# A graph layer on one core: the maxima of the turned tiles go to ScalarE, which then copies 84 columns a chunk, and the sums are cleared by a bitwise and

## The chip, the cores and the metric

One Trainium2 chip, one of its cores. The metric is the device time of one execution in microseconds (us); lower is better. The engines are named as in the profile: PE is TensorE (PEld its weight loads), DVE is VectorE, ACT is ScalarE, POOL is GpSimd, and SP is SyncE, which here only issues DMAs. Each engine runs its own instruction stream in order. The letter q behind an engine's name (ACTq, DVEq, SPq) marks what the engine's sequencer does by itself: it loads registers, waits for semaphores, issues DMAs, and hands the other instructions to the engine.

## The reference

One message-passing layer of a graph network. There are 12,500 nodes with 48 numbers each, and 400,000 edges with 32 numbers each; the edges are sorted by their destination.

```python
h = jnp.maximum(_layernorm(x, axis=-1), 0.0)
tmp = jnp.concatenate([h[dst], h[src], edge_attr], axis=1)     # 48 + 48 + 32
m = jax.nn.relu(tmp @ W1 + b1) @ W2 + b2                       # 128 hidden, 48 out
x = x + jax.ops.segment_sum(m, dst, num_segments=12500)
```

All of it is in fp32, and the output is the 12,500 x 48 array.

## The kernel before, in words

The first 95 us or so make the tables. The layer norm is applied, and the product with W1 is taken per node instead of per edge: `tab_a` has a row of 128 per node for the destination part, `tab_b` one for the source part, both in HBM. `bt` is `tab_b` turned, so that a node is a column of 128 partitions, and it stays in SBUF.

The main loop (`windows`) takes the edges in 391 chunks of 1024, a chunk being 8 tiles of 128 edges. For a chunk the kernel needs, edge by edge, the destination's row, the edge's own product and the source's row. The destinations of a chunk lie within 80 neighbouring nodes, so that a 0/1 matrix (`lhs`, made on DVE in L463), stacked on the edge numbers, gives the first two in one product with `rhs` (L481, into the PSUM tile `pre`). The sources are anywhere, and their rows come in one of three ways:

- most tiles: POOL gathers 128 rows of `tab_b` into `gb` by an indirect DMA (L452), and DVE adds them to `pre` (L517);
- the "turned" tiles: DVE and ACT copy 128 single columns of `bt` into a tile `gt`, one instruction per edge (L393), and PE adds the turned `gt` to `pre` (L491). A chunk has one or two turned tiles, 458 in all;
- 36 "single" tiles: SP issues one DMA per row into `gr` (L425), and DVE adds the tile (L515).

Then DVE takes the maximum with zero of the gathered tiles in place (`hidden`, L530, from `hid` to `hid`) and of the turned tiles (L532, from `pre` to `hid`). PE multiplies `hid` with a second 0/1 matrix `hot` (made in L469) and so folds a chunk into 80 columns (`fold`, L541; L546 counts the edges), and DVE adds these to a running array of sums `seg` in SBUF (`add`, L560). Every 12 chunks a segment of `seg` is done: PE multiplies it with W2 (L586, L587), DVE adds that to the node's `x` (L588), and SP stores it (L592). The array of the segment after next is cleared by two MEMSETs (L576), and the columns that reach over are copied (L578).

Which column a copy reads is a number in a register. `PARTS` sets how many columns are copied in a chunk, and by whom: four parts of 19, 20, 16 and 16 on DVE, five of 16 on ACT. Each part is a `load` followed by its `columns`: one TENSOR_LOAD on the engine's own sequencer brings the part's numbers from the SBUF tile `last` into registers (L358), and the copies behind it use them. Chunk c's numbers are in partition c % 128 of `last`. In part 0 the load brings one number more than the part's columns: where in `seg` the chunk adds.

The order of the work is written out by hand (`manual_schedule`), as a software pipeline. In round c of the loop, DVE does `lhs` and `hot` of chunk c, the addition and the maxima of chunk c-1, and the `add` of chunk c-2; PE does `before` (the product of L481) of chunk c-1, `fold` of chunk c-2 and `turned` (L491) of chunk c-1, in this order; the copies of round c fill the tiles that `turned` takes from round c+1 on. The `gt` pool has 5 buffers, so ACT may run some rounds ahead of the others until it needs a `gt` buffer that PE has not yet read.

Of the kernel before, what the change touches and what calls it, by code (L numbers as in the profile page):

```python
# [36 lines left out]
STORE = 2  # L37
# [33 lines left out]
SEG0 = 130848  # L71
# [207 lines left out]
def windows(nc, tc, gp, bt, ident, idx, x_t, tab_a, tab_b, dst, edge_t, w1, w2s, b2s, out_t):  # L279
# [3 lines left out]
    with ExitStack() as es:  # L283
# [54 lines left out]

        rhss = []
# [14 lines left out]
        def numbers(c, at, n, engine):  # L354

            got = []
            for k in range(0, n, MOST):
                got += nc.values_load_multi_w_load_instructions(  # L358
                    last[c % P : c % P + 1, c // P, at + k : at + min(k + MOST, n)],
# [40 lines left out]
        def mark(ins, us):  # L400
            marks.append((ins, us))
# [28 lines left out]
        def prepare(c):  # L430
# [9 lines left out]
            lhs = ld.tile([P, CE], F32, name="lhs")  # L440
# [67 lines left out]
        def gathered(c):  # L508

            s = st[c]  # L510
            s["h"] = h = wp.tile([P, T, HID], F32, name="hid")
# [7 lines left out]
            for fetch in s["fetches"]:  # L519
                tc.declare_no_dep(  # L520
                    added.ins, fetch, reason="the product that is waited for waits for the rows"
                )
            mark(added, 1.0)
            spans[c], marks[:] = list(marks), []

        def hidden(c):
# [3 lines left out]
            mark(nc.vector.tensor_scalar(of, of, 0.0, None, op0=ALU.max), 0.55)  # L530
            if turned_at(c):
                nc.vector.tensor_scalar(  # L532
                    apart(c, s["h"], True), apart(c, s["pre"], True), 0.0, None, op0=ALU.max
                )
# [35 lines left out]

        def segment_next(g):

            old, new = segs[g % 2], segs[(g + 1) % 2]
            if g > 0:
                for k in range(2):
                    nc.vector.memset(new[:, k, W:], 0.0)  # L576
# [401 lines left out]
```

## Time and profile before

| what | value |
|---|---|
| median of 3 runs | 3527.61 us (3528.13, 3527.61, 3518.28) |
| the profiled execution: time | 3517.03 us |
| the profiled execution: span from its first to its last instruction | 3515.3 us |
| DVE busy | 3234.7 us (92%) |
| ACT busy | 3123.3 us (89%) |
| POOL busy | 2660.5 us (76%) |
| PE busy | 2616.9 us (74%) |
| granted PE clock, mean | 0.781 |

A profiled execution is one run with the hardware profiler. In its rows "x" stands before a count; behind the bar come the time in which at least one instruction of the group ran, the mean length of one in ns, and the idle time of the engine just before them with what ended it. Single-column copies overlap one another on their engine, so that their mean length is more than the step from one start to the next. A register load on a sequencer is not counted as busy time, and where an engine stands still for one, the profile calls the wait "issue".

### The profile page before, as it was taken

How to read it: one execution, taken by the hardware profiler on the slowest of the kernel's cores; microseconds unless marked ns; L12 is line 12 of the kernel's file. 1: busy time of each engine (PE TensorE's matmuls, PEld its weight loads, DVE VectorE, ACT ScalarE, POOL GpSimd, SP SyncE). 2: the span in 40 equal slices, each digit the busy share in tenths (PEclk: the TensorE clock that was granted, in tenths of full speed). 3: DMA queues.
4: the chain of work that ended last, by engine and by line, in shares of the span. 5: the costliest groups of instructions: out<-in, count | busy, mean ns of one | idle time of the engine just before them, and what ended most of it. 6: DMA issues, size and time to landing. Idle time of an engine off the chain costs nothing.

```text
span 3515.3 us, 119801 instructions
## 1 busy us (share of the span) xinstructions
PE 2616.9 (74%) x17111; PEld 2351.3 (67%) x17111; DVE 3234.7 (92%) x30218; ACT 3123.3 (89%) x31115; POOL 2660.5 (76%) x2658
## 2 busy tenths in 40 slices
PE   8677777777777776777777777777777777777777
PEld 5567666666676666666666766666667666676666
DVE  6799999999999999999999999999999999999997
ACT  5899998999998899989999899899999999898893
POOL 5777777777777777777777777777777777777775
PEclk9777777778777778778877787777777778778777
DMA  5533333333333333333333333333333333333332
GB/s 198 169 98 99 95 94 95 93 93 104 96 96 93 93 95 98 97 95 94 96 94 94 100 96 94 95 93 94 103 96 95 93 93 96 97 100 97 92 94 68
DMA packets 197238, 349.02 MB, mean 99 GB/s; under 512 B 67762, under 2 KB 104516, under 8 KB 195156
## 3 DMA queue, kind: packets, MB, share of 16 engines
q0 software_dynamic: 84224, 172.62, 19.3%
q1 hardware_dynamic: 111952, 168.56, 16.1%
q14 instruction: 658, 5.39, 0.5%
q8 instruction: 144, 2.36, 0.3%
q10 hardware_dynamic: 260, 0.10, 0.0%
HBM read 321.55 MB, written 22.07 MB: 98 GB/s over the span
## 4 chain that ended last, share of the span: by engine, by line
DVE 75%; PE 10%; ACT 5%; issue 4%; DVEq 3%; ACTq 0%; DMA 0%; SPq 0%
DVE gt L393 40%; DVE hid L517 9%; DVE hot L469 7%; DVE lhs L463 6%; DVE hid L530 6%; ACT gt L393 5%; PE p_g L541 4%; DVEq L358 3%; DVE seg L560 2%; DVE hid L532 2%; PE p_f L586 2%; PE p_f L587 2%; DVE xseg L588 1%; PE pre L491 1%; DVE seg L576 1%
## 5 line engine op out<-in xcount | busy, mean ns | idle before, releaser
L393 ACT COPY gt<-bt 128x1 f32 x31040 | 3076.9, 187 | 298.9 <-PE pre L491 195.5
L452 POOL DMA_INDIRECT gb<-tab_b,srci x2631 | 2639.0, 1003 | 821.8 <-issue 373.3
L393 DVE COPY gt<-bt 128x1 f32 x27584 | 1813.3, 143 | 147.6 <-issue 98.3
L541 PE MATMUL p_g<-hot,hid 128*128 128x80 f32 x6250 | 1069.5, 342 | 839.5 <-DVE hid L530 838.5
L541 PEld LDWEIGHTS p_g<-hot,hid 128*128 128x128 f32 x6250 | 1001.1, 251 | 913.1 <-DVE hid L530 903.5
L481 PEld LDWEIGHTS pre<-rhs,lhs 112*128 112x128 f32 x6250 | 963.0, 243 | 92.1 <-issue 91.6
L481 PE MATMUL pre<-rhs,lhs 112*128 112x128 f32 x6250 | 989.7, 326 | 20.0 <-DMA lhs<-in_edge_t 17.4
L517 DVE TENSOR_TENSOR hid<-pre,gb 128x896 f32<-128x896 f32 (+2 forms) x391 | 408.0, 1044 | 0.0
L469 DVE TENSOR_TENSOR hot<-wnum,rel 128x640 f32<-128x640 f32 x391 | 318.2, 814 | 0.0
L463 DVE TENSOR_SCALAR lhs<-row,bw 80x1024 f32<-80x1024 int16 x391 | 289.7, 741 | 10.0 <-DMA row<-in_dst 10.0
L491 PE MATMUL pre<-ident,gt 128*128 128x128 f32 x916 | 271.3, 404 | 17.5 <-issue 12.1
L530 DVE TENSOR_SCALAR hid<-hid 128x896 f32<-128x896 f32 (+2 forms) x391 | 244.9, 626 | 0.1
L546 PE MATMUL p_g<-hot,ones 128*128 128x80 bf16 x3125 | 240.0, 238 | 0.0
L546 PEld LDWEIGHTS <-ones 128*128 128x128 bf16 x3125 | 239.9, 132 | 0.0
L491 PEld LDWEIGHTS pre<-ident,gt 128*128 128x128 f32 x916 | 193.1, 269 | 20.1 <-issue 14.3
L560 DVE TENSOR_TENSOR seg<-seg,p_g 128x160 f32 x391 | 122.4, 313 | 7.5 <-issue 3.5
L532 DVE TENSOR_SCALAR hid<-pre 128x128 f32<-128x128 f32 (+1 forms) x389 | 118.0, 303 | 0.0
L588 DVE TENSOR_TENSOR xseg<-xseg,p_f 48x512 f32<-48x512 f32 (+1 forms) x67 | 45.0, 672 | 63.9 <-PE p_f L587 63.8
L586 PE MATMUL p_f<-seg,w2s 128*48 128x512 f32 (+1 forms) x134 | 102.8, 861 | 0.4 <-DVE seg L560 0.4
L587 PE MATMUL p_f<-seg,b2s 1*48 1x512 f32 (+1 forms) x134 | 90.7, 763 | 0.0
L587 PEld LDWEIGHTS p_f<-seg,b2s 1*48 1x48 f32 x134 | 12.6, 137 | 84.3 <-issue 83.1
L576 DVE MEMSET seg<- 128x944 f32 x64 | 54.1, 845 | 9.3
(67 smaller groups left out, 289.4 us busy)
## 6 DMA issues: line engine op xcount, KB each, us to landing
gr<-tab_b SPq DMA_DIRECT2D x4608, 0.5 KB
row<-in_dst SPq DMA_DIRECT2D x390, 160.0 KB
lhs<-in_edge_t SPq DMA_DIRECT2D x390, 128.0 KB
gb<-tab_b,srci POOLq DMA_INDIRECT x2631
rhs<-tab_a SPq DMA_DIRECT2D x391, 40.0 KB
xseg<-in_x_t SPq DMA_DIRECT2D x33, 192.0 KB
out_x<-xseg SPq DMA_DIRECT2D x33, 192.0 KB
tab_b<-tab SPq DMA_DIRECT2D x3, 1280.0 KB
```

The source lines that it names most:

```text
L393: done = copy(gts[of][:, e : e + 1], bt8[:, bass.ds(at, 4)].bitcast(F32))
L452: fetch = nc.gpsimd.indirect_dma_start(out=gb[:, t, :], out_offset=None, in_=tab_b[:, :], in_offset=bass.IndirectOffsetOnAxis(ap=srci[:, c ...
L463: mark(nc.vector.tensor_scalar(lhs[:W, : n * P], row[:, : n * P], bw[:, c : c + 1], None, op0=ALU.is_equal,), 0.8)
L469: mark(nc.vector.tensor_tensor(hot[:, :n, :], wnum.unsqueeze(1).to_broadcast([P, n, W]), rel[:, c * T : c * T + n].unsqueeze(2).to_broadca ...
L481: s["behind"] = nc.tensor.matmul(pre[:, t, :], s["lhs"][:K, t * P : (t + 1) * P], s["rhs"][:K, :], start=True, stop=t not in turned_at(c), ...
L491: s["behind"] = nc.tensor.matmul(s["pre"][:, t, :], gts.pop(j), ident, start=False, stop=True).ins
L517: added = nc.vector.tensor_add(to, of, rows)
L530: mark(nc.vector.tensor_scalar(of, of, 0.0, None, op0=ALU.max), 0.55)
L532: nc.vector.tensor_scalar(apart(c, s["h"], True), apart(c, s["pre"], True), 0.0, None, op0=ALU.max)
L541: nc.tensor.matmul(p_g[:, 0, :], s["h"][:, t, :], s["hot"][:, t, :], start=t == 0, stop=t == n - 1)
L546: nc.tensor.matmul(p_g[:, 1, :], ones, high[:, t, 1::2], start=t == 0, stop=t == n - 1)
L560: mark(nc.vector.tensor_add(to, to, s["p_g"]), 0.25)
```

## The change

The maxima of the turned tiles leave DVE: `hidden` keeps the gathered tiles, and the new `hidden_turned` is an ACTIVATE with Relu on ACT, from `pre` to `hid`. It runs one round later, in round c for chunk c-2, just before `fold` of that chunk, and on ACT it stands behind the first of ACT's parts. `hid` and `lhs` become three fixed tiles each instead of pool buffers. The parts become 15, 20, 20 and 20 on DVE (75) and 20, 16, 16, 16 and 16 on ACT (84), 159 columns a chunk instead of 151; with them there are 483 turned tiles instead of 458, 48 single tiles instead of 36 (`SINGLE` rows a chunk go from 12 to 16), and 2594 gathered ones instead of 2631. The `gt` pool has 8 buffers instead of 5. The numbers lie in 64 partitions instead of 128: `row_of` uses the first 16 of each 32. The sums are cleared by a `tensor_scalar` with a bitwise and with 0, one half each in the sixth and the eighth round of a segment, instead of two MEMSETs in its last round. The product of a finished segment with W2 (`segment_product`) and its addition (`segment_sum`) are now in different rounds, the addition one round later, and the store comes two rounds later. Line numbers shift: in the changed kernel the copies are L407, the loads L372, the Relu L556.

```diff
 BLK = 512
-STORE = 2
+STORE = 4
+CLEAR = 5
...
 PARTS = (
-    (True, 0, 19, 1),
-    (True, 19, 20, 20),
-    (True, 39, 16, 40),
-    (True, 55, 16, 56),
-    (False, 71, 16, 72),
-    (False, 87, 16, 88),
-    (False, 103, 16, 104),
-    (False, 119, 16, 120),
-    (False, 135, 16, 136),
+    (True, 0, 15, 1),
+    (True, 15, 20, 16),
+    (True, 35, 20, 36),
+    (True, 55, 20, 56),
+    (False, 75, 20, 76),
+    (False, 95, 16, 96),
+    (False, 111, 16, 112),
+    (False, 127, 16, 128),
+    (False, 143, 16, 144),
 )
...
-SINGLE = 12
-SINGLE_AT = 160
+SINGLE = 16
+SINGLE_AT = 168
...
+HALF_ROWS = 16
+USED = P // 2
+LAST = (NCH + 2 + USED - 1) // USED
+
+
+def row_of(c):
+
+    group, row = divmod(c % USED, HALF_ROWS)
+    return 2 * HALF_ROWS * group + row, c // USED
...
-        gtp = es.enter_context(tc.tile_pool(name="gtp", bufs=5))
-        wp = es.enter_context(tc.tile_pool(name="wp", bufs=3))
+        ld = es.enter_context(tc.tile_pool(name="ld", bufs=LOADS))
+        gtp = es.enter_context(tc.tile_pool(name="gtp", bufs=8))
+        wp = es.enter_context(tc.tile_pool(name="wp", bufs=HIDS))
...
+        lhss = [one.tile([P, CE], F32, name=f"lhs{k}") for k in range(LOADS)]
+        hids = [one.tile([P, T, HID], F32, name=f"hid{k}") for k in range(HIDS)]
...
+            row, slot = row_of(c)
             for k in range(0, n, MOST):
                 got += nc.values_load_multi_w_load_instructions(
-                    last[c % P : c % P + 1, c // P, at + k : at + min(k + MOST, n)],
+                    last[row : row + 1, slot, at + k : at + min(k + MOST, n)],
...
-            s["h"] = h = wp.tile([P, T, HID], F32, name="hid")
+            s["h"] = h = hids[c % HIDS]
...
+            if c - HIDS in relus:
+                tc.declare_no_dep(
+                    added.ins, relus.pop(c - HIDS),
+                    reason="the products that read this buffer last waited for that maximum",
+                )
...
         def hidden(c):
 
             s = st[c]
             of = apart(c, s["h"], False)
             mark(nc.vector.tensor_scalar(of, of, 0.0, None, op0=ALU.max), 0.55)
+
+        def hidden_turned(c):
+
             if turned_at(c):
-                nc.vector.tensor_scalar(
-                    apart(c, s["h"], True), apart(c, s["pre"], True), 0.0, None, op0=ALU.max
-                )
+                relus[c] = nc.scalar.activation(
+                    apart(c, st[c]["h"], True), apart(c, st[c]["pre"], True), AF.Relu
+                ).ins
...
+        def segment_clear(g, k):
+
+            new = segs[(g + 1) % 2][:, k, W:].bitcast(I32)
+            nc.vector.tensor_scalar(new, new, 0, None, op0=ALU.bitwise_and)
+
         def segment_next(g):
 
             old, new = segs[g % 2], segs[(g + 1) % 2]
-            if g > 0:
-                for k in range(2):
-                    nc.vector.memset(new[:, k, W:], 0.0)
...
-        def segment_sum(g, k, n):
+        out_of = {}
+
+        def segment_product(g, k, n):
 
             seg, s = segs[g % 2], slice(k * BLK, k * BLK + n)
-            p_f = ps_f.tile([D, BLK], F32, name="p_f")
+            out_of[g, k] = p_f = ps_f.tile([D, BLK], F32, name="p_f")
             nc.tensor.matmul(p_f[:, :n], w2s, seg[:, 0, s], start=True, stop=False)
             nc.tensor.matmul(p_f[:, :n], b2s[:1, :], seg[:1, 1, s], start=False, stop=True)
-            nc.vector.tensor_add(xs[g][:, s], xs[g][:, s], p_f[:, :n])
+
+        def segment_sum(g, k, n):
+
+            s = slice(k * BLK, k * BLK + n)
+            nc.vector.tensor_add(xs[g][:, s], xs[g][:, s], out_of.pop((g, k))[:, :n])
...
                 load(c, 1)
                 columns(c, 1)
+                g, k = group(c - 2)
+                if g > 0 and k in (1, 3):
+                    segment_sum(g - 1, k // 2, BLK)
+                load(c, DVE_PARTS)
+                columns(c, DVE_PARTS)
                 if 0 <= c - 1 < NCH:
                     before(c - 1)
                 if 0 <= c - 2 < NCH:
+                    hidden_turned(c - 2)
                     fold(c - 2)
                 if 0 <= c - 1 < NCH:
                     turned(c - 1)
-
-                g, k = group(c - 2)
+                if g > 0 and k in (0, 2):
+                    segment_product(g - 1, k // 2, BLK)
                 if k == GQ - 3 or c == NCH - 1:
                     segment_load(g)
-                if g > 0 and k < L // BLK:
-                    segment_sum(g - 1, k, BLK)
                 if g > 0 and k == STORE:
                     segment_store(g - 1, L)
                 if 0 <= c - 1 < NCH:
...
                 columns(c, 2)
                 if 0 <= c - 1 < NCH:
                     hidden(c - 1)
+                if g > 0 and k in (CLEAR, CLEAR + 2):
+                    segment_clear(g, (k - CLEAR) // 2)
                 load(c, 3)
                 if 0 <= c - 2 < NCH:
                     add(c - 2)
                     if k == GQ - 1:
                         segment_next(g)
                 columns(c, 3)
-                for part in range(DVE_PARTS, len(PARTS)):
+                for part in range(DVE_PARTS + 1, len(PARTS)):
                     load(c, part)
                     columns(c, part)
                 if c == NCH + 1:
+                    segment_sum(g - 1, 1, BLK)
+                    segment_store(g - 1, L)
+                    segment_product(g, 0, END_L)
                     segment_sum(g, 0, END_L)
                     segment_store(g, END_L)
```

What is left out is the place of the columns in `last` and how the host fills it.

How the instructions stand, first on ACT in the middle of the main loop, three parts before (`gt` with a number is one of its buffers, `last` the numbers, `bt` the turned table):

```order
L393 COPY gt_73753<-bt_58 128x1 x16
L358 TENSOR_LOAD last_87
L393 COPY gt_74185<-bt_58 128x1 x16
L358 TENSOR_LOAD last_87
L393 COPY gt_74185<-bt_58 128x1 x16
```

and in the changed kernel, from the end of one round's copies to behind the Relu of the next round:

```order
L372 TENSOR_LOAD last_87
L407 COPY gt_71927<-bt_58 128x1 x16
L372 TENSOR_LOAD last_87
L407 COPY gt_71927<-bt_58 128x1 x14
L407 COPY gt_72264<-bt_58 128x1 x6
L556 ACTIVATE hid0_716<-pre_71681 128x2x128
L372 TENSOR_LOAD last_87
L407 COPY gt_72264<-bt_58 128x1 x16
```

The parts of 16 alternate with loads as before; new are the part of 20 (here 14 and 6, since a `gt` buffer is full) and the Relu between it and the next load (128x2x128 where the chunk has two turned tiles, 128x128 where it has one).

On DVE, from the addition of the gathered rows to the next chunk's `lhs`, before:

```order
L517 TENSOR_TENSOR hid_109192<-pre_109164,gb_108437 128x2x384
L358 TENSOR_LOAD last_87
L393 COPY gt_108981<-bt_58 128x1 x16
L530 TENSOR_SCALAR hid_109192<-hid_109192 128x2x384
L532 TENSOR_SCALAR hid_109192<-pre_109164 128x2x128
L358 TENSOR_LOAD last_87
L560 TENSOR_TENSOR seg0_663<-seg0_663,p_g_109173 128x2x80
L393 COPY gt_108981<-bt_58 128x1 x16
L463 TENSOR_SCALAR lhs_109545<-row_109547,bw_85 80x1024
```

and in the changed kernel:

```order
L531 TENSOR_TENSOR hid0_716<-pre_115878,gb_115056 128x2x384
L372 TENSOR_LOAD last_87
L407 COPY gt_115578<-bt_58 128x1 x20
L551 TENSOR_SCALAR hid0_716<-hid0_716 128x2x384
L372 TENSOR_LOAD last_87
L584 TENSOR_TENSOR seg0_663<-seg0_663,p_g_115888 128x2x80
L407 COPY gt_115578<-bt_58 128x1 x20
L477 TENSOR_SCALAR lhs2_715<-row_116234,bw_85 80x1024
```

One instruction is gone between the maximum and the load behind it, and both parts there have 20 copies instead of 16.

More of the change, by code (lines that the diff above doesn't have):

```diff
@@ L36 @@
 BLK = 512
-STORE = 2
+STORE = 4
+CLEAR = 5
+HIDS = LOADS = 3
 NOUT = NPAD + L
@@ L55 @@
 PARTS = (
-    (True, 0, 19, 1),
-    (True, 19, 20, 20),
-    (True, 39, 16, 40),
-    (True, 55, 16, 56),
-    (False, 71, 16, 72),
-    (False, 87, 16, 88),
-    (False, 103, 16, 104),
-    (False, 119, 16, 120),
-    (False, 135, 16, 136),
+    (True, 0, 15, 1),
[7 more added lines that the diff above has]
+    (False, 143, 16, 144),
 )
 PART = sum(n for _, _, n, _ in PARTS)
-BASE = 152
+BASE = 160
 DVE_PARTS = sum(dve for dve, *_ in PARTS)
 BT0 = 16512
-SEG0 = 130848
+SEG0 = 133248
 SEG_SIZE = 8 * L
-SEG, NEXT, SEG2 = 153, 154, 155
-PLACE0 = 156
-SINGLE = 12
-SINGLE_AT = 160
-WIDTH = 172
+SEG, NEXT, SEG2 = 161, 162, 163
+PLACE0 = 164
+SINGLE = 16
+SINGLE_AT = 168
+WIDTH = 184
 SLOTS = (NCH + 2 + P - 1) // P
 MOST = 32
+HALF_ROWS = 16
[4 more added lines that the diff above has]
+    return 2 * HALF_ROWS * group + row, c // USED
 def tiles_of(first, part):
@@ L287, in windows @@
         one = es.enter_context(tc.tile_pool(name="wone", bufs=1))
-        ld = es.enter_context(tc.tile_pool(name="ld", bufs=3))
-        gtp = es.enter_context(tc.tile_pool(name="gtp", bufs=5))
-        wp = es.enter_context(tc.tile_pool(name="wp", bufs=3))
+        ld = es.enter_context(tc.tile_pool(name="ld", bufs=LOADS))
+        gtp = es.enter_context(tc.tile_pool(name="gtp", bufs=8))
+        wp = es.enter_context(tc.tile_pool(name="wp", bufs=HIDS))
         grp = es.enter_context(tc.tile_pool(name="grp", bufs=3))
@@ L439, in prepare @@
             )
-            lhs = ld.tile([P, CE], F32, name="lhs")
+            lhs = lhss[c % LOADS]
             nc.sync.dma_start(lhs[W:K, : n * P], edge_t[:, at : at + n * P])
@@ L522, in gathered @@
                 )
+            if c - HIDS in relus:
[3 more added lines that the diff above has]
+                )
             mark(added, 1.0)
             spans[c], marks[:] = list(marks), []
+        relus = {}
         def hidden(c):
@@ L819, in tile_gnn_preln @@
     flag = const.tile([1, 1], I32, name="flag")
-    last = const.tile([P, SLOTS, WIDTH], I32, name="last")
+    last = const.tile([P, LAST, WIDTH], I32, name="last")
     ones = const.tile([P, P], BF16, name="ones")
@@ L924 @@
     by_tile = src.reshape(NT, P)
-    numbers = np.zeros((SLOTS * P, WIDTH), np.int32)
+    numbers = np.zeros((LAST * USED, WIDTH), np.int32)
     first = dst[::CE]
@@ L942 @@
     numbers[COLS : COLS + len(rows), SINGLE_AT : SINGLE_AT + SINGLE] = rows
-    last = np.ascontiguousarray(numbers.reshape(SLOTS, P, WIDTH).transpose(1, 0, 2))
+    last = np.zeros((P, LAST, WIDTH), np.int32)
+    for c, row in enumerate(numbers):
+        at, slot = row_of(c)
+        last[at, slot] = row
     arrays = {
```

## The prediction

> **What bounds the kernel now.** First the page: how busy each engine is, the chain that ended last, and the costliest groups.
>
> ```profile
> span 3515.3 us, 119801 instructions
> PE 2616.9 (74%) x17111; PEld 2351.3 (67%) x17111; DVE 3234.7 (92%) x30218; ACT 3123.3 (89%) x31115; POOL 2660.5 (76%) x2658
> DVE 75%; PE 10%; ACT 5%; issue 4%; DVEq 3%; ACTq 0%; DMA 0%; SPq 0%
> L393 ACT COPY gt<-bt 128x1 f32 x31040 | 3076.9, 187 | 298.9 <-PE pre L491 195.5
> ...
> L393 DVE COPY gt<-bt 128x1 f32 x27584 | 1813.3, 143 | 147.6 <-issue 98.3
> ```
>
> DVE carries the chain, and ACT is close behind it. Then the waits, to see which engine has slack, and for whom it waits.
>
> ```profile
> ACT gt L393 <- PE pre L491: 195.5, 89, 6.5
> ...
> DVE gt L393 <- issue: 98.3, 388, 3.6
> ...
> DVE xseg L588 <- PE p_f L587: 63.8, 37, 9.2
> ```
>
> DVE waits for another engine in the loop only at the segments' additions (63.8 us). ACT's slack is 195.5 us: in 89 places it has run so far ahead that no `gt` buffer is free. Over 390 rounds that is 0.50 us a round, and this is what an addition to ACT may cost before ACT sets the pace. Two rows of the timeline give DVE's pace:
>
> ```profile
> 105.65 0.75 DVE L463 TENSOR_SCALAR lhs<-row,bw 80x1024 f32<-80x1024 int16 x1 [9.09 <-DMA row<-in_dst]
> ...
> 3487.32 0.54 DVE L463 TENSOR_SCALAR lhs<-row,bw 80x640 f32<-80x640 int16 x1
> ```
>
> (3487.32 - 105.65) / 390 = 8.67 us a round. The question for the change is whether DVE or ACT needs longer for its new round.
>
> **ACT's round now.** Three views of ACT: its copies in two narrow stretches, an undisturbed stretch early in the loop, and its loads by stretches of time.
>
> ```profile
> 2005.44 1.11 ACT L393 COPY gt<-bt 128x1 f32 x11
> ...
> 2006.58 0.56 ACT L393 COPY gt<-bt 128x1 f32 x5
> ...
> 102.56 23.85 ACT L393 COPY gt<-bt 128x1 f32 x240 [0.17 <-issue]
> 126.58 0.56 ACT L393 COPY gt<-bt 128x1 f32 x5 [0.17 <-issue]
> ```
>
> ```profile
> L393 ACT COPY gt<-bt x31040: 185/187/193, 94.5 to 3464.9; 128x1 f32 x199
> ...
> L358 ACTq TENSOR_LOAD <-last x1: 1053/1053/1053, 2005.5 to 2005.5; - x1
> L358 ACTq TENSOR_LOAD <-last x56: 1047/1050/1376, 255.3 to 349.8; - x56
> L358 ACTq TENSOR_LOAD <-last x64: 1009/1022/1468, 369.1 to 479.5; - x64
> ```
>
> Eleven copies take 1.11 us, each 0.187, so the step is (1.11 - 0.187) / 10 = 0.0925 us. The last of them starts at 2006.365, the next at 2006.58, a step of 0.217: between them ACT stood still for the end of a load of 16 numbers, which began at 2005.46 with ten copies still to run and took 1.053. So a load is covered by ten instructions already handed over (0.925 us) and what is longer stalls the engine: 0.217 - 0.0925 = 0.12 us. The second fence has the loads of chunks whose numbers lie in the upper 16 of 32 partitions (1.050 us) and in the lower 16 (1.022). The stall of the lower ones, which alone the change uses, is therefore about 0.098. A round in the lower rows is 80 x 0.0925 + 5 x 0.098 = 7.89; measured over three undisturbed ones (126.58 - 102.56) / 3 = 8.01. The whole loop, with its first copy at 94.5 and its last ended at 3465.1, gives (3370.6 - 195.5) / 388 = 8.18 without the waits for PE, and 8.12 after taking off half the rows' 5 x 0.026. I take 8.06, between 8.01 and 8.12, since some loads of the long average are exposed by a wait in front of them.
>
> **What is added to ACT.** Four copies: 4 x 0.0925 = 0.37 us a round. The first part's load has 20 numbers instead of 16. ACT never loads 20 in this trace; DVE does, and SP loads 12:
>
> ```profile
> L358 DVEq TENSOR_LOAD <-last x1: 1387/1387/1387, 2001.3 to 2001.3; - x1
> ...
> L358 DVEq TENSOR_LOAD <-last x1: 1127/1127/1127, 2005.5 to 2005.5; - x1
> ...
> L358 SPq TENSOR_LOAD <-last x1: 787/787/787, 2001.8 to 2001.8; - x1
> ```
>
> 20 numbers take 1.387, 16 take 1.127, 12 take 0.787 on SP against ACT's 1.05 for 16: some 0.26 for four more on either. Ten copies cover no more than before, so all of it is stall: +0.26 us a round. Bounds: 0, if ACT's load does not grow, and 0.26; I take 0.26.
>
> The Relu has its nearest rows in the tables' part, the same function from PSUM to SBUF, in two lengths.
>
> ```profile
> L214 ACT ACTIVATE ht<-p_t 96x512 f32<-96x512 f32 x10 | 5.4, 581 | 0.0
> ...
> L214 ACT ACTIVATE ht<-p_t 96x256 f32<-96x256 f32 x3 | 1.1, 376 | 0.0
> ```
>
> 0.80 ns an element, so 128 elements take 0.274 us and 256 take 0.376. How it follows on other work shows in the same part of the timeline:
>
> ```profile
> 17.28 1.06 ACT L214 ACTIVATE ht<-p_t 96x512 f32<-96x512 f32 x2
> 18.24 1.06 ACT L234 COPY tab<-p_n 128x512 f32<-128x512 f32 x2
> ```
>
> The copy starts 0.10 before the Relu ends, as the single-column copies overlap by 0.187 - 0.0925 = 0.094. This leaves 0.18 for a chunk with one turned tile and 0.28 with two. With 483 turned tiles in 389 chunks 94 have two: 0.205 on average. The Relu is handed over just before the next load, in place of the tenth covering copy, and covers 0.18 instead of 0.0925 of it: that load's stall (0.098) shrinks by 0.09. Net +0.115; bounds 0.11 and, with no overlap and no cover, 0.30. What it waits for comes early: the sum of the gathered tiles (L531) of chunk c-2 is made in the middle of DVE's round c-1, some 5 us before ACT, at the same round, reaches the Relu of round c. So DVE may fall 5 us behind before ACT waits; the copies behind the Relu, and `fold` and L531 on the other side, would wait with it.
>
> The Trainium skill, "ScalarE: Activation LUTs", section "What ACT_TABLE_LOAD costs", gives 186 ns + 0.833 ns an element for an ACTIVATE with immediate scale and bias, and an overlap of 93 ns: an estimate from it is 0.20 us for one tile, 8 us more over the loop than my 0.18. Its section "Rules for kernel authors" says to use VectorE, not ScalarE, for relu and max, which speaks against this move; no run here shows the two against each other.
>
> ACT's round: 8.06 + 0.37 + 0.26 + 0.115 = **8.80 us**.
>
> **DVE's round.** It loses L532 and gains four copies.
>
> ```profile
> L532 DVE TENSOR_SCALAR hid<-pre 128x128 f32<-128x128 f32 x320 | 89.5, 280 | 0.0
> ...
> L532 DVE TENSOR_SCALAR hid<-pre 128x256 f32<-128x256 f32 x69 | 28.6, 414 | 0.0
> ```
>
> ```profile
> 2007.90 0.55 DVE L530 TENSOR_SCALAR hid<-hid 128x768 f32<-128x768 f32 x1
> 2008.37 0.42 DVE L532 TENSOR_SCALAR hid<-pre 128x256 f32<-128x256 f32 x1
> ...
> 2008.93 1.06 DVE L393 COPY gt<-bt 128x1 f32 x16
> ```
>
> (89.5 + 28.6) / 389 = -0.30. The copies step by (1.06 - 0.143) / 15 = 0.061, so +0.24. The wait for p_f goes, since the addition comes a round behind its product: 63.8 / 390 = -0.16. The stall for part 0's load ("issue", 98.3 / 390 = 0.25) goes, since that load now has 16 numbers behind a 0.74 us `lhs`. A new one comes: behind the maximum stands a load of 20 numbers (1.39) without L532 to cover it. Nine copies are 0.55, and the maximum holds DVE for some 0.5 (2007.90 to 2008.37 above), so `add` is 0.35 late. The bitwise and costs between 0.66 (as the SBUF-to-SBUF maximum, 0.55 for 768 columns) and 0.98 (one and a half times that) for a half where the MEMSET took 0.845:
>
> ```profile
> L576 DVE MEMSET seg<- 128x944 f32 x64 | 54.1, 845 | 9.3
> ```
>
> 64 of them are within 12 us either way, and they lie on an engine with slack. DVE: 8.67 - 0.30 + 0.24 - 0.16 - 0.25 + 0.35 = 8.55, less than ACT's 8.80.
>
> **The other engines.** POOL issues gathers from the start of the loop to its end:
>
> ```profile
> L452 POOL DMA_INDIRECT gb<-tab_b,srci x2631: 940/945/1783, 50.9 to 3491.0; - x188
> ```
>
> (3491.0 - 50.9) / 2630 = 1.308 us a gather; 2594 of them end at 3444, before ACT's end below. SP gets four more rows and a longer load a round. Its issues by line, its timeline and its waits:
>
> ```profile
> L436 SPq DMA_DIRECT2D rhs<-tab_a x391: 322/322/343, 95.1 to 3468.9; - x196
> ...
> 2002.70 4.28 SPq L425 DMA_DIRECT2D gr<-tab_b  x12
> ...
> SPq L592 <- DVE xseg L588: 438.5, 34, 30.9
> SPq L436 <- PE pre L481: 201.1, 95, 9.9
> ```
>
> (3468.9 - 95.1 - 438.5 - 201.1) / 390 = 7.0 us of work a round, and 4 x 4.28 / 12 + 0.26 = 1.7 more: 8.7. It stays under 8.80 and works ahead by three buffers, but it is the thinnest cover here. PE has 2616.9 / 391 = 6.7 a round. The three more `gt` buffers and the fixed `hid` and `lhs` tiles cost nothing and bring nothing: the Relu, not the buffers, now limits how far ACT runs ahead, to less than two rounds. The later store moves SP's 438.5 us of waiting, which lies where SP is ahead anyway.
>
> **The sum.** ACT now may not run ahead: its first Relu, in round 3, waits for chunk 1's addition:
>
> ```profile
> 124.17 1.08 DVE L517 TENSOR_TENSOR hid<-pre,gb 128x896 f32<-128x896 f32 x1
> ```
>
> That ends at 125.25. The rest of ACT's round 3 takes 6.6 and a once exposed load 0.9, so round 4 starts at 132.7. 385 rounds of 8.80 later, at 3520.7, round 389 starts; its Relu is at 3523. Then come PE's L546 and L491,
>
> ```profile
> 2012.00 0.74 PE L546 MATMUL p_g<-hot,ones 128*128 128x80 bf16 x8
> ...
> 2012.54 0.78 PE L491 MATMUL pre<-ident,gt 128*128 128x128 f32 x2
> ```
>
> 1.5 us with the last of fold's products, and 5 us on DVE from the addition through 40 copies to the copy into the next segment: 3530 for the last `lhs`. From there the end took 3515.3 - 3487.3 = 28.0; I take 25, since DVE no longer stands behind p_f there:
>
> ```profile
> 3502.08 0.68 DVE L588 TENSOR_TENSOR xseg<-xseg,p_f 48x512 f32<-48x512 f32 x1 [9.23 <-PE p_f L587]
> ```
>
> Span 3555, and with the 1.7 us around it 3557 us against the profiled execution's 3517: +1.1%. The median of the runs lies 10.6 us above that execution; I carry half of it: **3562 us**.
>
> **Rivals.** *ACT's loads stay covered (faster).* If a load of 20 costs ACT no more than one of 16, ACT's round is 8.54 and DVE's 8.55; the loop saves (8.67 - 8.55) x 390 = 47 us and POOL's last gather comes at 3444: some 3475. For it: no row has ACT loading 20. Against it: both other engines' loads grow by four numbers alike. Chance 0.13. *It comes out even.* With half of that stall the round is 8.67: 3510 to 3535; 0.10. *The Relu does not overlap.* At 0.30 net the round is 8.99: 386 x 0.185 = 71 us more, 3630. For it: it reads PSUM and changes the function between copies; against it: the overlap at 18.24. *DVE and ACT hold each other up*: fold waits for the Relu and L531 for `turned` behind it; a load after such a wait is exposed by 0.45, and DVE's 8.55 becomes 9.0, again about 3630. Against it: a DVE that falls behind by that no longer waits. Together 0.07.
>
> **How the numbers follow.** The forecast has 0.70, and its own range is 3535 to 3590 (0.05 us of a round is 20 us). A change under 0.3% (3517 to 3538) cannot be told from none here. Faster: 0.15; same 0.12; slower 0.73. The range of 3505 to 3605 leaves out the first rival and the top of the last two.
>
> **What would show it.** Right: ACT's idle time in front of L407 is "issue", with no wait for PE left; ACT's span of copies is about 8.8 a round; its loads show two lengths, 1.02 and 1.28; DVE's L531 waits for L505 on PE. Wrong: ACT waiting for DVE or PE at L556 in many rounds, loads of one length, or DVE without waits at 8.7 and more a round.

## The result, and the profile after

| kernel | median of 4 runs | lowest to highest |
|---|---|---|
| before | 3522.95 us | 3516.74 to 3528.13 |
| after the change | 3563.89 us | 3561.84 to 3567.18 |

The ratio of the changed kernel to the one before is 1.0118, with a 95% interval from 1.0095 to 1.0141: it is slower by about 41 us. The execution profiled took 3567.18 us.

First the page of the changed kernel: span, engines, chain and ACT's copies.

```profile
span 3565.5 us, 126262 instructions
PE 2668.1 (75%) x17161; PEld 2386.6 (67%) x17161; DVE 3242.2 (91%) x31432; ACT 3318.4 (93%) x33113; POOL 2620.9 (74%) x2621
DVE 65%; ACT 14%; PE 8%; issue 6%; DVEq 2%; ACTq 1%; SPq 0%; DMA 0%
L407 ACT COPY gt<-bt 128x1 f32 x32649 | 3219.3, 187 | 165.2 <-issue 147.9
```

ACT is now the busiest engine (3318.4 us, 195 us more than before), but DVE still carries the chain. Then the waits, one row each with the total in us, the number of times and the longest.

```profile
ACT gt L407 <- issue: 147.9, 550, 1.2
DVE seg L584 <- issue: 103.7, 315, 0.7
DVE gt L407 <- issue: 99.7, 414, 0.9
...
DVE hid L531 <- PE pre L505: 21.0, 15, 2.4
ACT hid L556 <- DVE hid L531: 18.4, 5, 10.8
...
DVE xseg L620 <- PE p_f L615: 3.1, 2, 1.7
```

ACT's 195.5 us of waiting for PE are gone. What is left in front of its copies is "issue", the ends of its own loads, and it waits for DVE in 5 places only. DVE no longer waits for p_f (3.1 us instead of 63.8), but a stall of the same kind as ACT's has appeared in front of the additions L584: 103.7 us. ACT's wait for DVE (18.4 us) and DVE's for the turned tiles (21.0 us) are both small. The pace of each comes from its first and last instruction (us, in the view of one line).

```profile
L477 DVE TENSOR_SCALAR lhs<-row,bw x391: 541/741/944, 107.2 to 3546.6; 80x1024 f32<-80x1024 int16 x195, 80x640 f32<-80x640 int16 x1
```

```profile
L556 ACT ACTIVATE hid<-pre x389: 261/266/383, 126.4 to 3548.5; 128x128 f32<-128x128 f32 x149, 128x256 f32<-128x256 f32 x46
```

DVE needs (3546.6 - 107.2) / 390 = 8.82 us a round, against 8.67 before. That is 0.15 x 390 = 59 us more. The end after the last `lhs` is shorter, 3565.5 - 3546.6 = 18.9 us instead of 28.0, and the first `lhs` comes 1.5 us later. Together this is the 50 us between the two spans. ACT's 389 Relus are (3548.5 - 126.4) / 388 = 8.82 us apart. So both engines run at one pace, and the profile alone does not say which of them sets it.

The new work on ACT, in its timeline and in the view of the loads of ACT and DVE (lengths of the shortest, the median and the longest in ns):

```profile
2000.09 1.95 ACT L407 COPY gt<-bt 128x1 f32 x20 [0.24 <-issue]
2001.95 0.27 ACT L556 ACTIVATE hid<-pre 128x128 f32<-128x128 f32 x1
2002.14 4.75 ACT L407 COPY gt<-bt 128x1 f32 x48
2007.06 1.58 ACT L407 COPY gt<-bt 128x1 f32 x16 [0.17 <-issue]
2008.89 1.95 ACT L407 COPY gt<-bt 128x1 f32 x20 [0.25 <-issue]
```

```profile
L372 ACTq TENSOR_LOAD <-last x1: 1260/1260/1260, 1998.8 to 1998.8; - x1
...
L372 DVEq TENSOR_LOAD <-last x1: 1360/1360/1360, 2000.4 to 2000.4; - x1
...
L372 ACTq TENSOR_LOAD <-last x1: 1024/1024/1024, 2001.0 to 2001.0; - x1
```

A load of 20 numbers takes 1.260 us on ACT, one of 16 takes 1.024; DVE's of 20 takes 1.360. The last of the 16 copies at 2007.06 starts at 2007.06 + 1.58 - 0.187 = 2008.45, the next copy at 2008.89. The step is 0.44, of which a copy would be 0.0925: the load of 20 stalls ACT for 0.35. The copy behind the Relu starts 0.19 after it, in place of 0.0925.

The new stalls on DVE, in its timeline:

```profile
2000.71 0.62 DVE L551 TENSOR_SCALAR hid<-hid 128x896 f32<-128x896 f32 x1
2001.84 0.32 DVE L584 TENSOR_TENSOR seg<-seg,p_g 128x160 f32 x1 [0.51 <-issue]
...
2004.87 0.81 DVE L483 TENSOR_TENSOR hot<-wnum,rel 128x640 f32<-128x640 f32 x1
2005.86 1.30 DVE L407 COPY gt<-bt 128x1 f32 x20 [0.19 <-issue]
...
490.51 0.67 DVE L620 TENSOR_TENSOR xseg<-xseg,p_f 48x512 f32<-48x512 f32 x1
492.44 0.96 DVE L531 TENSOR_TENSOR hid<-pre,gb 128x768 f32<-128x768 f32 x1 [1.26 <-PE pre L505]
```

Behind the maximum L551 the engine stands still for 0.51 us, until the load of 20 numbers for the last part has ended; behind `hot` it stands for 0.19. The last two rows are one of the places in which L531 waits for PE: those over half a us stand right behind the addition L620 of a finished segment.

### The profile page after: what moved, and what is told of

Read it like the earlier page. It is cut to its first block, busy times and chain, and to the rows that moved or that the text cites. A ratio compares the mean times of both kernels' runs of the same rounds, so it can differ in the third digit from the quotient of the medians.

```text
span 3565.5 us, 126262 instructions
## 1 busy us (share of the span) xinstructions
PE 2668.1 (75%) x17161; PEld 2386.6 (67%) x17161; DVE 3242.2 (91%) x31432; ACT 3318.4 (93%) x33113; POOL 2620.9 (74%) x2621
## 4 chain that ended last, share of the span: by engine, by line
DVE 65%; ACT 14%; PE 8%; issue 6%; DVEq 2%; ACTq 1%; SPq 0%; DMA 0%
DVE gt L407 37%; ACT gt L407 14%; DVE hid L531 8%; DVE hot L483 6%; DVE lhs L477 6%; DVE hid L551 5%; PE p_g L565 3%; DVE seg L584 2%; DVEq L372 2%; PE pre L495 2%; PE p_f L614 1%; PE p_f L615 1%; ACTq L372 1%; DVE seg L598 1%; DVE xseg L620 1%
## 5 line engine op out<-in xcount | busy, mean ns | idle before, releaser
L407 ACT COPY gt<-bt 128x1 f32 x32649 | 3219.3, 187 | 165.2 <-issue 147.9
L466 POOL DMA_INDIRECT gb<-tab_b,srci x2594 | 2599.4, 1002 | 868.6 <-issue 549.4
L407 DVE COPY gt<-bt 128x1 f32 x29175 | 1910.1, 143 | 121.3 <-issue 99.7
L565 PE MATMUL p_g<-hot,hid 128*128 128x80 f32 x6250 | 1088.5, 344 | 853.0 <-DVE hid L551 814.7
L565 PEld LDWEIGHTS p_g<-hot,hid 128*128 128x128 f32 x6250 | 1012.6, 252 | 932.3 <-DVE hid L551 879.6
L495 PE MATMUL pre<-rhs,lhs 112*128 112x128 f32 x6250 | 1004.9, 329 | 20.9 <-DMA gr<-tab_b 17.2
L531 DVE TENSOR_TENSOR hid<-pre,gb 128x896 f32<-128x896 f32 (+2 forms) x391 | 403.5, 1032 | 21.7 <-PE pre L505 21.0
L477 DVE TENSOR_SCALAR lhs<-row,bw 80x1024 f32<-80x1024 int16 x391 | 301.9, 772 | 11.1 <-DMA row<-in_dst 11.1
L551 DVE TENSOR_SCALAR hid<-hid 128x896 f32<-128x896 f32 (+2 forms) x391 | 239.4, 612 | 0.1
L584 DVE TENSOR_TENSOR seg<-seg,p_g 128x160 f32 x391 | 125.5, 321 | 107.2 <-issue 103.7
L505 PEld LDWEIGHTS pre<-ident,gt 128*128 128x128 f32 x966 | 202.5, 271 | 0.6 <-DVE gt L407 0.4
L556 ACT ACTIVATE hid<-pre 128x128 f32<-128x128 f32 (+1 forms) x389 | 113.3, 291 | 21.0 <-DVE hid L531 18.4
L620 DVE TENSOR_TENSOR xseg<-xseg,p_f 48x512 f32<-48x512 f32 (+1 forms) x67 | 44.7, 667 | 3.1 <-PE p_f L615 3.1
L598 DVE TENSOR_SCALAR seg<-seg 128x944 int32<-128x944 int32 x64 | 41.2, 644 | 0.0
```

Source lines behind the costliest of these rows:

```text
L407: done = copy(gts[of][:, e : e + 1], bt8[:, bass.ds(at, 4)].bitcast(F32))
L466: fetch = nc.gpsimd.indirect_dma_start(out=gb[:, t, :], out_offset=None, in_=tab_b[:, :], in_offset=bass.IndirectOffsetOnAxis(ap=srci[:, c ...
L477: mark(nc.vector.tensor_scalar(lhs[:W, : n * P], row[:, : n * P], bw[:, c : c + 1], None, op0=ALU.is_equal,), 0.8)
L495: s["behind"] = nc.tensor.matmul(pre[:, t, :], s["lhs"][:K, t * P : (t + 1) * P], s["rhs"][:K, :], start=True, stop=t not in turned_at(c), ...
L505: s["behind"] = nc.tensor.matmul(s["pre"][:, t, :], gts.pop(j), ident, start=False, stop=True).ins
L531: added = nc.vector.tensor_add(to, of, rows)
```

## Where DVE's round went

The steps from one DVE instruction's start to the next, summed over rounds 5 to 384 and sorted by the instruction that begins the step (us a round, worked out from the starts of all of DVE's instructions in each trace; `relu_dve` and `dve_12_8` are two of the experiments below):

```
step that begins with            before   after   relu_dve   dve_12_8
maximum of the gathered tiles    0.545    0.869   0.533      0.543
maximum of the turned tiles      0.250    -       0.428      -
lhs                              0.944    0.724   0.727      1.003
hot                              0.960    1.020   1.023      1.047
addition of the gathered rows    0.972    1.036   1.032      1.030
addition into seg                0.251    0.268   0.267      0.252
clear                            0.143    0.097   0.093      0.093
addition of a finished segment   0.101    0.161   0.164      0.149
copies of single columns         4.497    4.611   4.598      4.746
whole round, all steps           8.689    8.828   8.904      8.903
```

The step of the maximum now holds the stall that L532 covered before: 0.545 + 0.250 = 0.795 before, 0.869 after. The maxima of the turned tiles, 0.30 us of work, are gone from here, and this stretch of the round is still longer by 0.07, since the load behind it now brings 20 numbers instead of 16 and nothing covers its end.

## Experiments

The question is which engine sets the pace. Theory A, of the prediction: ACT does, and DVE has slack. Theory D: DVE does, at 8.8 us by its own loads, and ACT has slack. Theory L came with the first results: both stand at one level, so that relief of one alone gives little. Each run is compared with the kernel before on the same chip at the same time, which took 3522 to 3523 us there unless something else is said.

### The Relu back on DVE

The maxima of the turned tiles return to DVE, behind the maximum of the gathered ones; ACT keeps its 84 columns.

```diff
         def hidden(c):
...
+            if turned_at(c):
+                nc.vector.tensor_scalar(
+                    apart(c, s["h"], True), apart(c, s["pre"], True), 0.0, None, op0=ALU.max
+                )
         def hidden_turned(c):
 
-            if turned_at(c):
-                relus[c] = nc.scalar.activation(
-                    apart(c, st[c]["h"], True), apart(c, st[c]["pre"], True), AF.Relu
-                ).ins
+            pass
```

> The changed kernel with the maxima of the turned tiles back on DVE, behind the maximum of the gathered ones; ACT still copies 84 columns. Theory A (ACT sets the pace at 8.83 us a round, DVE is close behind at some 8.76): ACT loses the Relu and gets back the stall that the Relu covered, 8.71; on DVE the maximum's 0.25 comes back but covers the load of 20 behind it, so that the way from the maximum to add stays at 0.90 to 0.95 and DVE's round at 8.72 to 8.76. About 3530 us. Rival D (DVE sets the pace and the moved maxima were a gain of 0.30 a round for it): 3680 us.

Measured: 3592.33 us (3587.76 to 3597.12), 1.0194 times before, interval 1.0177 to 1.0211. This is 28 us more than the changed kernel, and both theories missed it. Its page's chain, two of its waits, DVE's line and DVE's timeline:

```profile
DVE 81%; PE 7%; issue 4%; DVEq 3%; SPq 1%; DMA 0%
```

```profile
ACT gt L407 <- PE pre L505: 59.7, 35, 6.1
...
DVE seg L585 <- issue: 27.3, 107, 0.5
```

```profile
L477 DVE TENSOR_SCALAR lhs<-row,bw x391: 539/741/939, 105.2 to 3573.9; 80x1024 f32<-80x1024 int16 x195, 80x640 f32<-80x640 int16 x1
```

```profile
2003.21 0.55 DVE L551 TENSOR_SCALAR hid<-hid 128x768 f32<-128x768 f32 x1
2003.67 0.42 DVE L553 TENSOR_SCALAR hid<-pre 128x256 f32<-128x256 f32 x1
2004.46 0.32 DVE L585 TENSOR_TENSOR seg<-seg,p_g 128x160 f32 x1 [0.37 <-issue]
```

ACT, with 84 columns and no Relu, has slack again (it waits 59.7 us for PE), and DVE sets the pace at (3573.9 - 105.2) / 390 = 8.89 us. The maximum L553 takes 0.42 here, but the stall behind it is 0.37 instead of 0.51, and on average the stalls in front of the addition fall from 103.7 to 27.3 us. So the Relu's move is worth 8.89 - 8.82 = 0.07 to 0.08 us a round to DVE, not 0.30: most of L532's time lay beside a load. The Trainium skill's advice in "ScalarE: Activation LUTs", "Rules for kernel authors", to leave relu to VectorE, does not hold in the changed kernel: with these parts VectorE is the worse place for it by 28 us, and for two tiles the instruction takes 0.42 us there and 0.37 on ScalarE.

### Relief for ACT alone: 80 columns, or loads of 12

```diff
-    (False, 75, 20, 76),
-    (False, 95, 16, 96),
-    (False, 111, 16, 112),
-    (False, 127, 16, 128),
-    (False, 143, 16, 144),
+    (False, 75, 16, 76),
+    (False, 91, 16, 92),
+    (False, 107, 16, 108),
+    (False, 123, 16, 124),
+    (False, 139, 16, 140),
```

> The changed kernel with ACT's first part cut from 20 columns to 16, so 80 columns a chunk on ACT, 155 in all; DVE as it is. Theory A: ACT's round falls by 0.37 + 0.31 to about 8.2 and DVE's own 8.76 sets the pace: about 3537 us, with DVE's waits for PE L505 gone. If DVE needed only the 8.55 of the prediction it would be 3455 to 3480. Rival D: DVE sets the pace already, 3564 us as with the change.

The other keeps 84 columns on ACT and cuts them in seven loads of 12.

```diff
-    (False, 75, 20, 76),
-    (False, 95, 16, 96),
...
-    (False, 143, 16, 144),
+    (False, 75, 12, 76),
+    (False, 87, 12, 88),
...
+    (False, 147, 12, 148),
```

> The changed kernel with ACT's 84 columns in seven parts of 12 instead of 20 and four of 16. Theory A with the price of a load read as its time beyond ten covering copies: a load of 12 takes 0.77 us, less than 0.925, so the stalls at the parts (0.39 + 0.18 + 3 x 0.12 a round) nearly vanish, ACT's round is 8.0 to 8.2, and DVE's 8.76 sets the pace: about 3537 us, as with 80 columns. If the stall is a price per load instead, seven loads cost more than five: 3600 us and more. Rival D: 3564 us.

Measured: with 80 columns 3566.63 us (3556.58 to 3573.46), 1.0116 [1.0096, 1.0135]; with loads of 12, 3559.45 us (3551.84 to 3566.0), 1.0097 [1.0081, 1.0114]. Both intervals overlap that of the changed kernel, so neither has gained anything that can be told. The rows of each, first with 80 columns, then with loads of 12 (its lines have numbers higher by two):

```profile
ACT hid L556 <- DVE hid L531: 58.9, 50, 11.5
```

```profile
L477 DVE TENSOR_SCALAR lhs<-row,bw x391: 540/741/941, 106.3 to 3549.7; 80x1024 f32<-80x1024 int16 x195, 80x640 f32<-80x640 int16 x1
```

```profile
ACT hid L558 <- DVE hid L533: 65.2, 63, 12.9
```

```profile
L374 ACTq TENSOR_LOAD <-last x6: 783/785/798, 2000.4 to 2006.0; - x6
```

```profile
2001.22 6.83 ACT L409 COPY gt<-bt 128x1 f32 x72 [0.20 <-issue]
2007.95 0.27 ACT L558 ACTIVATE hid<-pre 128x128 f32<-128x128 f32 x1
2008.39 3.74 ACT L409 COPY gt<-bt 128x1 f32 x39 [0.17 <-issue]
```

The loads of 12 do what was priced: one takes 0.785 us, less than ten copies take, and 72 copies with their loads step by (6.83 - 0.187) / 71 = 0.094 us, so that nothing is stalled there. Not every stall of ACT is gone, though: in places a load is still exposed, as the 0.20 and 0.17 in the rows show, and "issue" in front of its copies is 167.7 us over the run. In both it is now ACT that waits for DVE, in 50 and 63 places instead of 5. But DVE needs (3549.7 - 106.3) / 390 = 8.83 us a round with ACT relieved. So DVE by itself is enough to hold the time of the changed kernel. Theory A expected a gain in both runs; there is none, as theory D has it.

### A smaller last load on DVE

The part of 20 columns whose load stalls DVE behind the maximum becomes 12 and 8.

```diff
-    (True, 55, 20, 56),
+    (True, 55, 12, 56),
+    (True, 67, 8, 68),
...
                 columns(c, 3)
+                load(c, 4)
+                columns(c, 4)
```

> The changed kernel with DVE's last part of 20 columns cut into 12 and 8, so that the load behind the maximum has 12 numbers; ACT as it is. Theory A: the way from the maximum to add falls from 0.94 to 0.6 to 0.7 and DVE's own round to about 8.5, but ACT's 8.83 stays: 3555 to 3565 us, with DVE waiting 80 us or more for PE L505. Rival D: DVE sets the pace, and 0.25 a round is 97 us: 3467 us.

Measured: 3595.39 us (3587.2 to 3596.08), 1.0199 [1.0182, 1.0216], and again both theories missed. DVE's line, its wait for loads and its timeline:

```profile
L478 DVE TENSOR_SCALAR lhs<-row,bw x391: 540/741/971, 106.7 to 3575.5; 80x1024 f32<-80x1024 int16 x195, 80x640 f32<-80x640 int16 x1
```

```profile
DVE gt L408 <- issue: 221.1, 882, 0.7
```

```profile
2000.70 0.74 DVE L478 TENSOR_SCALAR lhs<-row,bw 80x1024 f32<-80x1024 int16 x1
2001.67 1.00 DVE L408 COPY gt<-bt 128x1 f32 x15 [0.23 <-issue]
```

The stall behind the maximum has gone (its step is 0.543 in the table, from 0.869), but the stall in front of part 0 has come back: the step of `lhs` is 1.003, from 0.724, and the copies take 0.13 more. The fifth load stands behind only 12 copies, and part 0's load behind only 8 and `lhs`. So the latter begins late: 0.22 us or three copies before `lhs` starts, where it is 0.55 us or nine copies in the changed kernel (medians, worked out from the starts in the two traces). DVE needs (3575.5 - 106.7) / 390 = 8.89 us. A stall that is cut in one place stood up again in the next, and the extra load was added to it.

### 71 columns on DVE

Relief for DVE alone: its last part becomes 16 (71 columns, as before the change), and ACT keeps its parts of 20 and 16.

```diff
-    (True, 55, 20, 56),
-    (False, 75, 20, 76),
-    (False, 95, 16, 96),
-    (False, 111, 16, 112),
-    (False, 127, 16, 128),
-    (False, 143, 16, 144),
+    (True, 55, 16, 56),
+    (False, 71, 20, 72),
+    (False, 91, 16, 92),
+    (False, 107, 16, 108),
+    (False, 123, 16, 124),
+    (False, 139, 16, 140),
```

> The changed kernel with DVE's last part cut from 20 columns to 16 (71 on DVE, ACT's 84 as with the change), for a chip where the kernel before takes 3523 us. Theory L: ACT's own round is 8.80 us whatever DVE does, so 3545 to 3565 us although DVE needs 8.3 to 8.5, with DVE waiting 100 us or more for PE L505 behind the Relu. Rival D (DVE alone sets the pace of the change): about 3490 us, as with 71 and 80 columns.

Measured: 3547.74 us (3545.37 to 3561.59), 1.0089 [1.0063, 1.0114]. The chain, the two lines, DVE's wait and one of PE's:

```profile
ACT 58%; DVE 22%; PE 6%; issue 5%; ACTq 3%; DVEq 1%; SPq 0%; DMA 0%
```

```profile
L556 ACT ACTIVATE hid<-pre x389: 261/266/384, 124.8 to 3526.2; 128x128 f32<-128x128 f32 x155, 128x256 f32<-128x256 f32 x40
```

```profile
L477 DVE TENSOR_SCALAR lhs<-row,bw x391: 544/740/957, 106.2 to 3521.9; 80x1024 f32<-80x1024 int16 x195, 80x640 f32<-80x640 int16 x1
```

```profile
DVE hid L531 <- PE pre L505: 81.2, 67, 2.9
```

```profile
PE p_g L565 <- ACT hid L556: 201.8, 152, 3.4
```

The chain has gone over to ACT, and DVE waits for the product of the turned tiles (81.2 us instead of 21.0). On PE that product stands behind `fold`, and `fold` waits for ACT's Relu: 201.8 us, against 36.2 in the changed kernel. ACT's own round is (3526.2 - 124.8) / 388 = 8.77 us. Relief of DVE alone gains some 16 us by the medians (the intervals still overlap), and then ACT holds. Theory D, by which ACT has slack, falls here; theory L is left: ACT stands only 0.05 us a round below DVE.

### 71 columns on DVE and 80 on ACT

Both are relieved: the parts are 15, 20, 20, 16 on DVE and five of 16 on ACT. These are 151 columns, as before the change, though DVE's 71 are divided otherwise; all else of the change stays.

```diff
-    (True, 55, 20, 56),
-    (False, 75, 20, 76),
-    (False, 95, 16, 96),
-    (False, 111, 16, 112),
-    (False, 127, 16, 128),
-    (False, 143, 16, 144),
+    (True, 55, 16, 56),
+    (False, 71, 16, 72),
+    (False, 87, 16, 88),
+    (False, 103, 16, 104),
+    (False, 119, 16, 120),
+    (False, 135, 16, 136),
```

> The changed kernel with both reliefs (71 columns on DVE, 80 on ACT), for a chip where the kernel before takes 3523 us. Theory L (DVE and ACT at one level with the change): DVE's own round 8.3, ACT's 8.2 to 8.3, so the pace is POOL's: 2619 gathers of 1.31 to 1.33 us end at 3482 to 3534, and some 23 more to the end: 3505 us, range 3480 to 3555. Rival D (DVE alone sets the pace, and more than these steps): 3560 us, as with the change.

Measured: 3495.08 us (3492.21 to 3496.93), 0.9925 [0.9909, 0.9942]: faster than both kernels.

```profile
DVE 64%; SPq 12%; issue 7%; PE 6%; DMA 4%; DVEq 3%
```

```profile
L477 DVE TENSOR_SCALAR lhs<-row,bw x391: 543/741/962, 105.5 to 3470.4; 80x1024 f32<-80x1024 int16 x195, 80x640 f32<-80x640 int16 x1
```

```profile
ACT hid L556 <- DVE hid L531: 47.4, 45, 11.8
DVE lhs L477 <- DMA row<-in_dst: 45.6, 49, 8.3
...
DVE seg L584 <- issue: 14.2, 45, 0.5
```

DVE needs (3470.4 - 105.5) / 390 = 8.63 us, and its stall in front of the addition is 14.2 us instead of 103.7, as the last load has 16 numbers. So the change without its eight columns is worth 27 us over the kernel before, and the eight columns cost 69 us. No run tells which share of the 27 us belongs to the Relu, the later additions, the clear or the other parts. By the medians, and taken alone, the four on DVE cost 72 us here (act80 against this run, 3566.63 - 3495.08) and the four on ACT 53 us (dve71_c against this run): the two prices do not add, as theory L says. What comes next is the row transfers that SP issues: `lhs` waits for them for 45.6 us, and SP has 12% of the chain.

### Six runs under another pace

Before these two, the same kernels (dve71 and dve71_act80, each twice), one with 71 columns on DVE and ACT's 84 in loads of 12, and the changed kernel with the MEMSET in place of the bitwise and were run at times when the chip took 4484 to 4489 us for the kernel before as well; they are compared with that alone.

```diff
         def segment_clear(g, k):
-            new = segs[(g + 1) % 2][:, k, W:].bitcast(I32)
-            nc.vector.tensor_scalar(new, new, 0, None, op0=ALU.bitwise_and)
+            nc.vector.memset(segs[(g + 1) % 2][:, k, W:], 0.0)
```

> The changed kernel with DVE's last part cut from 20 columns to 16 (71 on DVE, 84 on ACT). Theory L (two engines at one level: DVE's own round is 8.81 to 8.83 us and ACT's is 8.80, so that relief of either alone leaves the time as it is): DVE's round falls by 4 copies, 0.24, and by the stall behind the maximum, some 0.27, to 8.3; ACT's 8.80 stays: 3545 to 3560 us, with DVE waiting for PE L505. Rival D (DVE alone sets the pace, ACT needs clearly less): the next limit is POOL with 2607 gathers, 3485 to 3500 us.

> The changed kernel with both reliefs: DVE's last part and ACT's first part at 16 (71 and 80). Theory L: DVE 8.3, ACT 8.2, so the pace is POOL's or SP's: 2619 gathers of 1.31 from 51 us on end at 3482, and some 23 more to the end: about 3505 us, range 3480 to 3515. If ACT relief did nothing (rival D) it equals the run with 71 columns on DVE alone, but for the 12 gathers more (16 us).

> The changed kernel with 71 columns on DVE (last part 16) and ACT's 84 in seven parts of 12. Theory L with stalls priced as the load's time beyond ten copies: ACT's round is 8.0 to 8.2, DVE's 8.3, POOL's 2607 gathers end at 3465: 3485 to 3500 us. If what costs on ACT is the columns and not the load's stall, it stays with the run with 71 columns and the old ACT parts: 3545 to 3560 us.

> The changed kernel with the sums cleared by a MEMSET of each half in the same rounds, instead of the bitwise and. A half takes 845 ns then, 644 now: 64 x 0.2 = 13 us on DVE, unless the stall of the load behind it hides it. Theory L: 3564 to 3577 us. If ACT alone set the pace: 3564 us.

> The changed kernel with DVE's last part cut from 20 columns to 16 (71 on DVE, 84 on ACT), once more, on a chip where the kernel before takes its usual 3523 us. Theory L (two engines at one level: DVE's own round is 8.81 to 8.83 us and ACT's is 8.80, so that relief of either alone leaves the time as it is): DVE's own round falls to 8.3; ACT's 8.80 stays: 3545 to 3560 us, with DVE waiting for PE L505. Rival D (DVE alone sets the pace, ACT needs clearly less): 3485 to 3500 us, with POOL's gathers as the next limit.

> The changed kernel with both reliefs (71 columns on DVE, 80 on ACT), once more, on a chip where the kernel before takes its usual 3523 us. Theory L: DVE 8.3, ACT 8.2 to 8.3, so the pace is POOL's or SP's: 2619 gathers of 1.31 to 1.33 us from 51 us on end at 3482 to 3534, and some 23 more to the end: 3505 us, range 3480 to 3555. Rival D: as the run with 71 columns on DVE alone, but for the 12 gathers more (16 us).

Measured, as ratios to the kernel before at that time: dve71 1.0276 [1.0247, 1.0305] and again 1.028 [1.0263, 1.0297]; dve71_act80 1.0079 [1.0049, 1.0109] and again 1.0088 [1.0072, 1.0105]; dve71_act84_12s 1.0215 [1.0185, 1.0245]; memset 1.0131 [1.0102, 1.016]. From the profile of dve71, two waits:

```profile
ACT gt L407 <- issue: 926.6, 2308, 4.7
DVE gt L407 <- issue: 748.9, 1636, 2.8
```

The same program had 137.0 and 160.1 us of these in dve71_c. On ACT and DVE the single instructions have the same length in both (the copies on ACT 187 ns, the loads 1.024 and 1.026 us at the median). PE differs: its granted clock is 0.660 against 0.763, and its products for the turned tiles take 457 ns against 408. In dve71, 829 of the 1762 pauses of over 0.25 us in front of ACT's copies end within 0.06 us of such a pause of DVE, where chance would give 67; in dve71_c it is none of 112 (from the starts in the traces, from 200 us on). So what holds back the instructions seems to act on both engines at once, and the order of the kernels changes with it: dve71_act80 is slower than the kernel before there and faster here. These six do not bear on which engine sets the pace at 3523 us, and what holds the issue back stays open. They show nothing on the MEMSET either, since the changed kernel was not run beside it; its own row gives the length alone:

```profile
L597 DVE MEMSET seg<- 128x944 f32 x64 | 54.1, 845 | 9.5 <-issue 0.7
```

## Why the prediction was right and where it was wrong

**The time and its sign were right**: 3562 us forecast, 3563.89 measured. That they lie 2 us apart is luck: the sum gave 3557 us for a profiled execution, which took 3567.18, and the 5 us added for the median made up for part of it, though the median lay 3 us below the profiled execution this time. **ACT's round was right**, 8.80 us forecast; where ACT sets the pace (dve71_c) it is 8.77, and its terms were found one by one. The load of 20 numbers takes 1.26 us against 1.28, and the step over it 0.44 against 0.0925 + 0.098 + 0.26 = 0.45. A Relu of one tile takes 0.266 us against 0.274, and the copy follows 0.19 behind it against 0.18. The rule that ten handed-over instructions cover a load fits the loads of 12, which are shorter than that and stall nothing between the copies. The estimate from the Trainium skill ("ScalarE: Activation LUTs", section "What ACT_TABLE_LOAD costs") was 0.20 for that step; the trace's 0.19 lies between the two forecasts. The wait of the first Relu for chunk 1's addition was right too (126.4 us against 125.25 and a little).

**The step that failed is DVE's round**: "8.55, less than ACT's 8.80". It is 8.82. By the terms of that sum, with the table above:

- L532 taken off and the load behind the maximum exposed: -0.30 + 0.35 = +0.05 forecast, +0.07 measured. Right.
- Four copies: +0.24 forecast. The copies' steps grew by 0.114, with the p_f wait (which the table holds in the copies ahead of it) gone from them: 63.8 - 3.1 us over 390 rounds are 0.16, so the copies themselves are about +0.27. Near enough.
- Part 0's stall: -0.25 forecast, -0.22 measured. Right.
- Not in the sum: +0.06 behind the addition of the gathered rows. The third part went from 16 to 20 numbers too, and its load takes 1.36 us now against 1.12. Where it begins eight or more copies before the addition it is still covered: DVE then stands still for over 0.05 us in 1 of 245 rounds. With fewer copies in front it is not: DVE stands still in 96 of 135 such rounds, against 17 of 132 before (from the starts in the two traces).
- Not in the sum: +0.06 behind the addition of a finished segment. This is the 21.0 us for which L531 now waits for PE (0.05 a round), nearly all of it behind L620, in places of which the timeline above shows one. So the p_f wait of 63.8 us went, and a wait a third as long stands one instruction later.
- Not in the sum: +0.06 behind `hot`, where a load of 20 stood before the change as well. By the starts in the two traces this load now begins 0.44 us (seven copies) before `hot` instead of 0.55 us (nine), and in both kernels the next copy starts 0.09 us after it has ended. That it begins later because part 0 in front of it has only 15 copies instead of 19 fits the late load behind the 8 copies of dve_12_8, but no run changes part 0 alone.
- The clear: no effect forecast; its step is 0.05 shorter.

With the smaller rows these add up to +0.14, the change of the whole round in the table. So where the prediction said "ACT sets the pace", DVE and ACT were level within 0.05 us. The number came out because ACT's round was right, and DVE's happened, by luck, to be the same. The sign that the prediction named against itself, "DVE without waits at 8.7 and more a round", is what came; the chain (DVE 65%, ACT 14%) pointed to it, and act80 and act84_12s, where ACT is relieved and the time stays, showed it.

**The other steps.** "Issue" in front of ACT's copies and no wait for PE: right. POOL was no limit, as forecast: its last gather starts at 3498.4 (3444 forecast, at 1.308 us a gather; they came at 1.329, held by the others).

```profile
L466 POOL DMA_INDIRECT gb<-tab_b,srci x2594: 938/944/1947, 52.6 to 3498.4; - x200
```

SP, "the thinnest cover", shows no wait of DVE for its rows beyond the first few rounds; it comes to the fore only at 8.63 us a round, in the fastest kernel. The tail was 18.9 us from the last `lhs`, not 25, but that `lhs` came at 3546.6 us, not at 3530: the span is 10 us longer than the forecast one.

**The rivals.** "ACT's loads stay covered" fell with the load of 1.26. It would not have saved 47 us in any case: with ACT's loads covered (act84_12s) DVE held 3559 us. "It comes out even" fell with the step of 0.44, which is the whole stall and not half of it. "The Relu does not overlap" fell with the 0.19. "DVE and ACT hold each other up" fell with the 18.4 and 21.0 us of waits between them.

## What to carry to other kernels

Where two engines stand close, work out the round of the second as carefully as that of the first, load by load: here one was right and the other 0.27 us off, and only relief of both together (3495 us) gained anything worth having. An instruction that is taken off an engine saves only what did not lie beside something else: 0.30 us of maxima were worth 0.08, as a register load's end came in its place. More columns for each engine, and a cheaper round, were two changes in one; run apart, the second gains 27 us and the first costs 69. And cutting a part smaller can move a stall instead of removing it: count how many instructions stand between one register load and the next (dve_12_8).

## What the runs showed of the hardware that was not expected

- A register load on ACT takes 0.785 us for 12 numbers, 1.024 for 16 and 1.260 for 20: about 0.06 a number. DVE needs 1.36 for 20.
- The bitwise and over a half of the sums takes less time than the MEMSET of the same size, 845 ns above, though it reads what it writes:

```profile
L598 DVE TENSOR_SCALAR seg<-seg 128x944 int32<-128x944 int32 x64 | 41.2, 644 | 0.0
```

- The same program took 3548 and 4608 us at different times, with instructions of the same length on ACT and DVE, a granted clock of 0.66 instead of 0.76, and nearly seven times as much "issue" in front of ACT's copies. Nearly half of these pauses end together with one of DVE's. What makes it so was not found.
